# A two-layer graph network kernel: Wf's loads and W's rows in another order, and background work that passes a transposition waiting for banks

## The chip, the cores and the metric

The kernel runs on one core of one Trainium2 chip. The metric is the device time of one execution in microseconds; a kernel's time is the median of several runs.

## The reference

x has 2708 rows of 1024 float32 values, adj is a 2708 x 2708 matrix of int32. All weights are 1024 x 1024, and all arithmetic is float32.

```python
# layer 0
h = jnp.maximum(_layernorm(x, axis=-1), 0.0)
f = h @ Wf + bf
g = h @ Wg + bg
e = jax.nn.relu(f @ g.T)
scores = jnp.where(adj > 0, e, NEG)
attention = jax.nn.softmax(scores, axis=1)
x = x + attention @ (h @ W + bW)
# layer 1
h = jnp.maximum(_layernorm(x, axis=-1), 0.0)
hW = h @ W1
e = leaky_relu(hW @ a1 + (hW @ a2).T, 0.2)
scores = jnp.where(adj > 0, e, neg)
x = x + relu(jax.nn.softmax(scores, axis=1) @ hW)
```

## The kernel before

**Tiles and stages.** The rows are cut into tiles of 128, two tiles make a pair; there are ten pairs (0 to 9) and a unit of leftover rows (LEFT). The columns of the score matrix are cut into five panels of four tiles and some leftover columns. Every large product is made with seven products of half-sized blocks in place of eight, named M1 to M7; sums and differences of the operands are made on VectorE, and a product's result is read out of PSUM by one engine and combined.

Layer 0 doesn't make f and g apart: M = Wf Wg^T is made once, and the scores are h M h^T plus vectors. For the first panel the stages are, with the lines where their matmuls stand: transposes of Wg (L555) and Wf (L579) and M's rows (L591), 0 to 150 us; q = M times the panel's h (`project_q`, matmul at L679, results in the banks qx, qy, qz), 150 to 208 us; scores of all pairs against the panel (L1425, banks sx, sy, sz, the pair's h read back from DRAM as As), 208 to 374 us; then the next panel's q, 374 to 430 us; the softmax; the aggregate (L679 again, banks gx, gy, gz, gv, h read back as hc), 430 to 586 us; the projection with W (L1314), 588 to 636 us. The next panels and layer 1 follow.

**Background work.** While PE makes M and the first q, the other engines prepare h pair by pair. `make_pairs` puts these items for each pair into a list `later`: two normalizations (their fetch loads 16 pieces of x), one that stores the rows to hg_d (L143), the transposition (16 transposes on PE at L457 into four banks h_ps, copied by ACT to four tiles hsT), two dot products with the vector vb, and sums of hsT which are stored to hs_d. An item has a cost, a fetch, what it does, whether it takes PSUM banks, and a condition. `behind(us, psum_free)` is called in between the matmuls: it adds `us` to a credit and runs items from the head of the list while there is credit. An item that takes banks isn't run where `psum_free` is false, and then nothing behind it is either. `one` runs the head and starts the fetches of the next items. In the first q, the banks are free behind M1, M2, M7 and M4 only. `prepare_W` (L1352) puts eight items into the same list: W's rows (w_rows, loaded on ACT's queue) are summed on DVE into the operands wt_d of the projection; the layer-1 items also make dot products with a1 and a2 (the tiles wab).

**Queues.** `load` (L139) issues on SP, `store` (L143) on POOL's queue, w_rows on ACT's; each queue issues in program order and waits in that order. L45 is a helper through which all DVE and ACT work goes in a set order. r is the vector of the dot products; when a panel's four tiles are done, `columns_to_row` (L275) writes their column of r to DRAM as r_d, one float of 4 bytes at a time, on POOL's queue; the scores read it as a row. For the loads there is one pool of twelve buffers, shared by wg, wf, hsT, the mask tiles adj_i, As, hc and w_rows, taken in turn: a load waits until the last user of its buffer is done.

**Wf.** Four of Wf's eight row blocks are loaded at the start. In the loop over rows of M (L622), row i + 4 is loaded when row i is transposed, two per turn, and the pair loads of x come between on SP.

Of the kernel before, what the change touches and what calls it, by code (L numbers as in the profile page):

```python
# [57 lines left out]
def kernel(  # L58
# [21 lines left out]
    NC = D // P  # L80
# [117 lines left out]
    ahead = [5]  # L198
    spare, from_slots = [False], [False]

    def put(us, go, fetch=None, takes_psum=False, ready=None, to=later):
        to.append([us, fetch, go, takes_psum, ready])

    def one(of=None):
        of = later if of is None else of
        for it in of[:4 if of is lazy and from_slots[0] else ahead[0]]:
            if it[1]:
                it[1]()
                it[1] = None
        us, _, go = of.pop(0)[:3]  # L210
        go()
        return us

    def behind(us, psum_free=False):
        credit[0] = min(credit[0] + us, 2 * us)
        while later and credit[0] > 0 and (psum_free or not later[0][3]) and (not later[0][4] or later[0][4]()):
            credit[0] -= one()
        while spare[0] and not later and lazy and credit[0] > 0:
            credit[0] -= one(lazy)

# [220 lines left out]
    def make_pairs():  # L441
        xs, hT = {}, {}

        def fetch(q):
            xs[q] = []
            for t in units[q]:
                xs[q].append(row_halves("x"))
                load_rows_of(t, xs[q][-1], x)
# [58 lines left out]
        def bias(q, k):  # L507
            dots(q, k)
            drop(q, f"dots{k}")

        seen = {}
        def put_norms(q):
            put(2.1, lambda: normalize(xs[q][0]), lambda: fetch(q))
            put(2.1, lambda: normalize(xs[q][1]))

        put_rows = lambda q: put(0.5, lambda: rows(q))
        def put_dots(q):
            for k in range(2):
                put(1.6, lambda k=k: bias(q, k), ready=lambda: vb[0] is not None)

        todo = [0, 1, LEFT] + list(range(2, NQ))
        put_norms(todo[0])
# [97 lines left out]
    nc.hold = ("vector", "scalar")  # L620
    transposed_wg(0, ws)
    for a in range(NC):  # L622
        for i in range(2 * a, min(2 * a + 2, NC)):
            if i + 4 < NC:
                rows_of_wf[i + 4] = load_rows(wf, i + 4, "wf")
            transposed_wf(i)
        half_row_of_M(a, 0)
        if a == NH:
            dot(c0, halves(bfb), halves(bgb))
            vb = [slot(f"vb{g}") for g in range(2)]  # L630
            for g in range(2):
                spread(vb[g][:, :W], [v[:, 4 * g + j:4 * g + j + 1] for j in range(4)])
            ws = fetch_wg(1)
        bias_of_g(a, ws)
        if a == NH + 2:
            transposed_wg(1, ws)
        behind(2.0 if a < NH else 5.0, True)
        if a == 1:
            nc.hold = ()
# [610 lines left out]
    def project(l, p, G, finish, then={}, by_pair=False, rate=2.0):  # L1250
# [10 lines left out]
        start_of, join, finish = finish  # L1261

        order = (M1, M5, M2, M6, M7, M3, M4) if by_pair else (M1, M2, M5, M6, M3, M7, M4)
        ws = {m: load_W(l, m) for m in order[:2]}
        start_of([t for g in todo for t in g[:2]] + ([other] if other else []))
        def left_of(ta, tb, one, two):
            (a11, a12), (a21, a22) = one, two
# [84 lines left out]
    def prepare_W():  # L1352
        ab, rows = [], {}

        def fetch(l, k):
            if l == 1 and not ab:
                for k2, a in enumerate((a1, a2)):
                    row_to_all(a, wab[k2])
                ab.extend(halves(t) for t in wab)
            rows[l, k] = [load_rows(w_in[l], c, "w_rows", by_scalar) for c in (k, k + NH)]  # L1360

        def go(l, k):
            two = rows.pop((l, k))
            if l == 1:
                for i, c in enumerate((k, k + NH)):
                    for j in range(2):
                        dot(wa[:, j, c:c + 1], halves(two[i]), ab[j])
            right_of_W(l, k, *two)

        for l in range(2):  # L1370
            for k in range(NH):
                put(2.7 if l == 0 else 8.0, lambda l=l, k=k: go(l, k), lambda l=l, k=k: fetch(l, k))

    def spread_wa():
        for k in range(2):
# [156 lines left out]
    def softmax(p, S, m):  # L1532

        w = width[p]
        mb, sm = slot("mb"), slot("sm")
        spread(mb, columns_of(p, m))

        def step(q, k):
            s = S[units[q][k]]
            sub(s[:, :w], s[:, :w], mb[:, :w])  # L1540
            nc.scalar.activation(s[:, :w], s[:, :w], AF.Exp)

        order = order_of_units
        exps[0] = 0

        def go(i):
            if i < len(order):
                step(*order[i])
            if i >= LAG:
                q, k = order[i - LAG]  # L1550
                total(p, sm, S[units[q][k]], once(q, k), i == LAG)
            exps[0] += 1
        later[:0] = [[1.4, None, (lambda i=i: go(i)), False, None] for i in range(len(order) + LAG)]
        return sm

    def shifts1(p, between=None):
# [211 lines left out]
    for p in range(NP):  # L1768
        got["S"], got["acc"] = scores(p, B)
        generated[p] = NQ + 1  # L1770
        ahead[0] = 2
        S = got["S"]
        hooks = {M1: lambda p=p: take_max(p), M2: lambda p=p: take_softmax(p)}
        if p == 0:
            hooks[M1] = lambda: (held(take_max, 0), sums_may.__setitem__(0, True), sums_until(3))
        if p + 1 < NP:
            B = project_q(p + 1, hooks)
        else:
            nc.hold = ("vector",)
            project(0, p - 1, G.pop(p - 1), finish0(p - 1), hooks)  # L1780
            nc.hold = ()
            scores_before()
        then = {M4: lambda: (sums_until(NQ), prepare_W())} if p == 0 else {}
        ahead[0] = 1 if p == 0 else 2
        if p == NP - 2:
            then[M2] = lambda: first_masks(NP - 1, 0)
            then[M6] = lambda: first_masks(NP - 1, 1)
            then[M7] = lambda: first_masks(NP - 1, 2)
        spare[0], from_slots[0] = p > 0, p == NP - 1
        G[p] = aggregate(0, p, S, got["sm"], then)  # L1790
        spare[0] = False
        if p == 0:
            flush()
            ahead[0] = 2
            for s in range(1, NP):
                columns_to_row(r_d[s], s, r_[:, first_col[s]:])
            spread_wa()
        if p < NP - 2:
            project(0, p, G.pop(p), finish0(p), {M1: lambda p=p: first_masks(p + 1, 0),
                                                 M5: lambda p=p: first_masks(p + 1, 1),  # L1800
                                                 M7: lambda p=p: first_masks(p + 1, 2)})
# [4 lines left out]
    def weights1(p, z, m, shift):  # L1806
# [46 lines left out]
        for i in range(len(order) + LAG):  # L1853
            mk = []
            front.append([2.1, (lambda i=i, mk=mk: mk.append(load_mask(p, *order[i])))
                          if i < len(order) and not (p == 0 and units[order[i][0]][order[i][1]] in before) else None,
                          (lambda i=i, mk=mk: go(i, mk)), False, None])
        later[:0] = front
        return S, sm

# [89 lines left out]
```

## Time and profile before

| what | us |
|---|---|
| time, median of 3 runs | 3054.39 (3045.55 to 3057.21) |
| the profiled execution | 3049.19 |
| its span | 3047.3 |
| PE busy in the span | 2993.9 |
| DVE busy | 2047.6 |
| ACT busy | 536.8 |
| POOL busy | 496.9 |

The profile is of one execution, with a time of its own between the runs above. PE is TensorE's matmuls, DVE VectorE, ACT ScalarE, POOL GpSimd and SP the engine that only issues loads. A timeline line has a start and a duration in us, the engine, the line of the code, the operation with the tile written and the tiles read, and in brackets how long the engine had been idle and what ended that. A windows line has, for a stretch of time, the sum and the busy time of PE, its weight loads, DVE, ACT and POOL (with the number of instructions), the granted clock, the share of time in which the DMA engines were busy, and GB/s. A chain of waits is followed back from an instruction to what released it.

### The profile page before, as it was taken

How to read it: one execution, taken by the hardware profiler on the slowest of the kernel's cores; microseconds unless marked ns; L12 is line 12 of the kernel's file. 1: busy time of each engine (PE TensorE's matmuls, PEld its weight loads, DVE VectorE, ACT ScalarE, POOL GpSimd, SP SyncE). 2: the span in 40 equal slices, each digit the busy share in tenths (PEclk: the TensorE clock that was granted, in tenths of full speed). 3: DMA queues.
4: the chain of work that ended last, by engine and by line, in shares of the span. 5: the costliest groups of instructions: out<-in, count | busy, mean ns of one | idle time of the engine just before them, and what ended most of it. 6: DMA issues, size and time to landing. Idle time of an engine off the chain costs nothing.

```text
span 3047.3 us, 41722 instructions
## 1 busy us (share of the span) xinstructions
PE 2993.9 (98%) x14642; PEld 2294.2 (75%) x14642; DVE 2047.6 (67%) x4667; ACT 536.8 (18%) x880; POOL 496.9 (16%) x770
## 2 busy tenths in 40 slices
PE   8998999999999999999999999999999999999999
PEld 4576777667877588885888886784767959879695
DVE  5776794585742686616965276867878768887863
ACT  4420020020200121101210111302232121212200
POOL 1421111210112110223111111131212010020201
PEclk9999999999999999999999999999999999999999
DMA  6989878887466786768957588679768768878887
GB/s 232 302 271 272 311 276 308 264 286 235 133 236 165 228 273 195 247 156 251 292 188 251 179 241 258 223 292 335 245 212 264 263 202 299 294 265 297 264 294 268
DMA packets 392704, 766.78 MB, mean 252 GB/s; under 512 B 65728, under 2 KB 206944, under 8 KB 392464
## 3 DMA queue, kind: packets, MB, share of 16 engines
q1 hardware_dynamic: 332336, 584.80, 59.6%
q0 software_dynamic: 54464, 164.78, 16.1%
q10 hardware_dynamic: 5696, 14.55, 1.4%
q8 instruction: 116, 1.90, 0.2%
q14 instruction: 92, 0.75, 0.1%
HBM read 630.04 MB, written 138.11 MB: 252 GB/s over the span
## 4 chain that ended last, share of the span: by engine, by line
PE 73%; DVE 11%; issue 8%; DMA 5%; POOL 1%; ACT 1%; SPq 1%; POOLq 0%; DVEq 0%; ACTq 0%
PE sz L1425 6%; PE gy L679 6%; PE gz L679 6%; PE gz L1114 5%; PE gx L679 5%; PE sx L1425 4%; PE pz L1314 4%; PE sy L1425 4%; PE px L1314 4%; PE py L1314 3%; PE gy L1114 3%; PE gx L1114 3%; PE gv L679 3%; PE M_ps L591 3%; PE qz L679 2%
## 5 line engine op out<-in xcount | busy, mean ns | idle before, releaser
L1425 PE MATMUL sz<-B,As 128*128 128x288 f32 (+2 forms) x1200 | 292.0, 392 | 6.0 <-DVE st L45 5.1
L1425 PEld LDWEIGHTS sz<-B,As 128*128 128x128 f32 x1200 | 227.2, 190 | 55.2 <-DVE st L45 8.4
L1425 PE MATMUL sx<-B,As 128*128 128x288 f32 (+2 forms) x800 | 200.8, 394 | 12.4 <-DMA As<-hs_d 10.4
L1425 PE MATMUL sy<-B,As 128*128 128x288 f32 (+2 forms) x800 | 199.0, 392 | 0.0
L1425 PEld LDWEIGHTS sx<-B,As 128*128 128x128 f32 x800 | 152.5, 191 | 45.8 <-DMA As<-hs_d 9.5
L679 PE MATMUL gz<-Sa,hc 128*128 128x288 f32 (+2 forms) x800 | 185.8, 392 | 0.0
L679 PEld LDWEIGHTS gz<-Sa,hc 128*128 128x128 f32 x800 | 151.5, 190 | 32.2 <-issue 2.2
L1425 PEld LDWEIGHTS sy<-B,As 128*128 128x128 f32 x800 | 151.7, 190 | 30.6 <-DVE st L45 0.3
L1114 PE MATMUL gz<-quarter,hc 128*128 128x128 f32 (+2 forms) x1344 | 168.8, 279 | 3.8 <-DVE gT L45 3.7
L1114 PEld LDWEIGHTS gz<-quarter,hc 128*128 128x128 f32 x1344 | 160.6, 191 | 5.1 <-DVE gT L45 4.6
L143 POOL DMA_DIRECT2D out_dram<-x_res x164 | 81.2, 502 | 469.1 <-DVE x_res L45 461.9
L1314 PE MATMUL py<-w,ps 128*128 128x512 f32 x320 | 142.0, 593 | 0.0
L1314 PE MATMUL pz<-w,ps 128*128 128x512 f32 x320 | 142.0, 594 | 0.0
L1314 PE MATMUL px<-w,gT 128*128 128x512 f32 x320 | 141.1, 593 | 0.0
L679 PE MATMUL gy<-T,hc 128*128 128x288 f32 (+2 forms) x480 | 114.9, 402 | 3.8 <-DMA hc<-hg_d 3.8
L1314 PEld LDWEIGHTS pz<-w,ps 128*128 128x128 f32 x320 | 60.2, 190 | 76.2 <-issue 72.2
L1314 PEld LDWEIGHTS py<-w,ps 128*128 128x128 f32 x320 | 60.5, 190 | 75.1 <-issue 72.7
L591 PE MATMUL M_ps<-wgT,wfT 128*128 128x512 f32 x256 | 112.7, 596 | 1.6 <-ACT hsT L45 1.6
L1314 PEld LDWEIGHTS px<-w,gT 128*128 128x128 f32 x320 | 60.1, 190 | 71.3 <-issue 67.8
L679 PEld LDWEIGHTS gy<-T,hc 128*128 128x128 f32 x480 | 93.1, 194 | 24.7 <-DMA hc<-hg_d 4.3
L143 POOL DMA_DIRECT2D mk_d<-mask x55 | 35.9, 654 | 456.4 <-DVE mask L45 439.4
L45 ACT ACTIVATE P<-P 128x576 f32<-128x576 f32 (+3 forms) x111 | 72.1, 650 | 207.3 <-DVE P L45 207.2
(391 smaller groups left out, 5819.6 us busy)
## 6 DMA issues: line engine op xcount, KB each, us to landing
hc<-hg_d SPq DMA_DIRECT2D x175, 512.0 KB
As<-hs_d SPq DMA_DIRECT2D x150, 512.0 KB
hc<-hr_d SPq DMA_DIRECT2D x119, 512.0 KB
hc<-hs_d SPq DMA_DIRECT2D x112, 512.0 KB
w<-wt_d SPq DMA_DIRECT2D x96, 512.0 KB
w<-in_L_gnn_W_dram SPq DMA_DIRECT2D x72, 512.0 KB
md<-md_d SPq DMA_DIRECT2D x56, 512.0 KB
adj_i<-in_adj_dram SPq DMA_DIRECT2D x200, 128.0 KB
```

What stands on the lines that cost most here:

```text
L45: i = f(*a, **k)
L143: nc.gpsimd.dma_start(a, b)
L591: nc.tensor.matmul(ps, wfT[a][c // NH][:, c % NH, :], wgT[b][c], start=(c == 0), stop=(c == NC - 1))
L679: nc.tensor.matmul(ps[d], left(m, k, d), right(m, k), start=(start and k == 0), stop=(k == K - 1), skip_group_check=True)
L1114: nc.tensor.matmul(ps[:, d], lhs[:, d * P:(d + 1) * P], inner_right(m, n, k), start=(start and k == 0 and d == 0), stop=(k == NK - 1), ski ...
L1314: nc.tensor.matmul(ps, left[i][m][:, k, :], w_[k], start=(start and k == 0), stop=(k == NH - 1), skip_group_check=True)
L1425: nc.tensor.matmul(ps[:n, :h], lefts[q][:, i % 2, c, :n], B[m][c // 2][:, c % 2, :h], start=(start and c == 0), stop=(c == NH - 1), skip_g ...
```

## The change

It has four parts. Rows 4 to 7 of Wf are loaded together in the first turn of the loop, and row 0 of M is made as soon as row block 0 is transposed, before row block 1. Normalizations and dot products are marked `apart`; when the head of the list takes banks and none are free, `behind` runs the first of the next seven items that is marked and has been fetched. `prepare_W` is put behind M2 of the first panel's aggregate, not M4, and its layer-0 items cost 5.4, not 2.7. The first projection loads three of its weights ahead of the x_res tiles, not two. The other lines of the diff give the items that are put in by hand the new field.

```diff
-    def put(us, go, fetch=None, takes_psum=False, ready=None, to=later):
-        to.append([us, fetch, go, takes_psum, ready])
+    def put(us, go, fetch=None, takes_psum=False, ready=None, to=later, apart=False):
+        to.append([us, fetch, go, takes_psum, ready, apart])
 
-    def one(of=None):
+    def one(of=None, n=0):
         of = later if of is None else of
         for it in of[:4 if of is lazy and from_slots[0] else ahead[0]]:
             if it[1]:
                 it[1]()
                 it[1] = None
-        us, _, go = of.pop(0)[:3]
+        us, _, go = of.pop(n)[:3]
         go()
         return us
 
     def behind(us, psum_free=False):
         credit[0] = min(credit[0] + us, 2 * us)
-        while later and credit[0] > 0 and (psum_free or not later[0][3]) and (not later[0][4] or later[0][4]()):
-            credit[0] -= one()
+        while later and credit[0] > 0:
+            may = lambda it: (psum_free or not it[3]) and (not it[4] or it[4]())
+            n = 0
+            if later[0][3] and not may(later[0]):
+                n = next((i for i, it in enumerate(later[:7]) if it[5]), 0)
+                if n == 0 or later[n][1]:
+                    break
+            if not may(later[n]):
+                break
+            credit[0] -= one(n=n)
...
         def put_norms(q):
-            put(2.1, lambda: normalize(xs[q][0]), lambda: fetch(q))
-            put(2.1, lambda: normalize(xs[q][1]))
+            put(2.1, lambda: normalize(xs[q][0]), lambda: fetch(q), apart=True)
+            put(2.1, lambda: normalize(xs[q][1]), apart=True)
...
-                put(1.6, lambda k=k: bias(q, k), ready=lambda: vb[0] is not None)
+                put(1.6, lambda k=k: bias(q, k), ready=lambda: vb[0] is not None, apart=True)
...
     for a in range(NC):
+        if a == 0:
+            for i in range(4, NC):
+                rows_of_wf[i] = load_rows(wf, i, "wf")
         for i in range(2 * a, min(2 * a + 2, NC)):
-            if i + 4 < NC:
-                rows_of_wf[i + 4] = load_rows(wf, i + 4, "wf")
             transposed_wf(i)
-        half_row_of_M(a, 0)
+            if a == i:
+                half_row_of_M(a, 0)
+        if a:
+            half_row_of_M(a, 0)
...
-        ws = {m: load_W(l, m) for m in order[:2]}
+        ws = {m: load_W(l, m) for m in order[:3 if l == 0 and p == 0 else 2]}
...
-                put(2.7 if l == 0 else 8.0, lambda l=l, k=k: go(l, k), lambda l=l, k=k: fetch(l, k))
+                put(5.4 if l == 0 else 8.0, lambda l=l, k=k: go(l, k), lambda l=l, k=k: fetch(l, k))
...
-        then = {M4: lambda: (sums_until(NQ), prepare_W())} if p == 0 else {}
+        then = {M2: lambda: (sums_until(NQ), prepare_W())} if p == 0 else {}
```

More of the change, by code (lines that the diff above doesn't have):

```diff
@@ L1552, in go @@
             exps[0] += 1
-        later[:0] = [[1.4, None, (lambda i=i: go(i)), False, None] for i in range(len(order) + LAG)]
+        later[:0] = [[1.4, None, (lambda i=i: go(i)), False, None, False] for i in range(len(order) + LAG)]
         return sm
@@ L1856, in weights1 @@
                           if i < len(order) and not (p == 0 and units[order[i][0]][order[i][1]] in before) else None,
-                          (lambda i=i, mk=mk: go(i, mk)), False, None])
+                          (lambda i=i, mk=mk: go(i, mk)), False, None, False])
         later[:0] = front
```

## The prediction, made before the changed kernel had run

> **What bounds the kernel now.** I read the page first, then the waits of PE, then the places of the longest waits in the timeline, then DVE and SP around them.
>
> ```profile
> PE 2993.9 (98%) x14642; PEld 2294.2 (75%) x14642; DVE 2047.6 (67%) x4667; ACT 536.8 (18%) x880; POOL 496.9 (16%) x770
> PE 73%; DVE 11%; issue 8%; DMA 5%; POOL 1%; ACT 1%; SPq 1%; POOLq 0%; DVEq 0%; ACTq 0%
> PE sx L1425 <- DMA As<-hs_d: 10.4, 2, 9.0
> PE gy L679 <- DMA hc<-hg_d: 3.8, 1, 3.8
> PE wT_ps L579 <- DMA wf<-in_L_gnn_Wf_dram: 3.0, 2, 1.8
> PE wT_ps L579 <- ACT x L45: 1.1, 1, 1.1
> ```
>
> PE is busy in 2993.9 of 3047.3 us, so all its idle time is 53.4 us, and the change takes no matmul away. Whatever it gains is one of these waits and the slow clock after it. The last four lines (reason, total, times, longest) are the ones that the change can touch.
>
> ```profile
> 39.33 1.06 PE L579 MATMUL wT_ps<-ident,wf 128*128 128x128 f32 x8 [1.22 <-DMA wf<-in_L_gnn_Wf_dram]
> 41.45 1.94 PE L579 MATMUL wT_ps<-ident,wf 128*128 128x128 f32 x8 [1.05 <-ACT x L45]
> 43.18 14.69 PE L591 MATMUL M_ps<-wgT,wfT 128*128 128x512 f32 x32
> 182.87 7.92 PE L679 MATMUL qy<-hT,ms 128*128 128x288 f32 x32
> 235.51 2.10 PE L1425 MATMUL sy<-B,As 128*128 128x288 f32 x8
> 246.61 3.65 PE L1425 MATMUL sx<-B,As 128*128 128x288 f32 x8 [9.00 <-DMA As<-hs_d]
> 489.58 4.15 PE L679 MATMUL gv<-Sb,hc 128*128 128x288 f32 x16
> 513.06 7.18 PE L679 MATMUL gy<-T,hc 128*128 128x288 f32 x16 [3.81 <-DMA hc<-hg_d]
> ```
>
> Start, duration, what, and in brackets the idle time. Three places wait: Wf's last rows at 39 and 41, the third pair of the scores at 246, the last group of M5 in the aggregate at 513. After each the same matmuls run slower (3.65 against 2.10, 7.18 against 4.15). The line at 182.87 doesn't wait in this kernel; it is where I expect the change to make a new wait.
>
> ```profile
> 176.11 1.51 DVE L45 TENSOR_TENSOR m<-qy,m 128x288 f32<-128x288 f32 x4
> 197.76 1.28 DVE L45 BATCH_NORM_STATS2 bn<-x 128x6 f32<-128x512 f32 x2
> 181.92 7.40 SPq L139 DMA_DIRECT2D x<-in_x_dram  x16
> 140.00:150.00 10.00, 10.00 (x36) 5.31 (x35) 7.24 (x21) 4.53 (x9) 5.08 (x9) 1.00 1.05 407
> 150.00:160.00 10.00, 10.00 (x51) 8.16 (x50) 9.07 (x17) 6.25 (x12) 2.71 (x5) 1.00 1.03 187
> ```
>
> The first reads M5 out of the four qy banks; the second normalizes pair 8's first tile; the third loads pair 8. The windows end in GB/s: 407, and 187 after r_d's 4-byte column was issued at 146.72. In the chain of waits before 246.61:
>
> ```profile
> 219.45 0.76 POOL r_d L275
> 220.20 4.72 issue
> 224.95 0.50 POOL hs_d L143
> 225.48 9.64 DMA hs_d<-hsT
> 240.20 6.37 DMA As<-hs_d
> ```
>
> r_d lies between pair 7's stores, the last of them takes 9.64 us, SP then loads masks into the buffer it frees, and only then As.
>
> **What the Trainium skill says.** "TensorE: Matmul & The Clock Gate", section "What's actually happening": after an idle window of about 3.4 us the array runs at half clock until about 3.4 us of work. The trace agrees: the 9.00 us wait costs 1.55 more, the 3.81 us one 3.03 more. "DMA: Bandwidth & Descriptors", section "Specifications": below 512 B a DMA does a read-modify-write. The two r_d writes that I looked at alone landed 10.4 and 11.7 us after their issue, and in the windows 221 to 224 us, just after another, nothing moves at all (0 GB/s).
>
> **The change part by part**, against the profiled execution (3049.19 us; the median shown, 3054.39, is 5.2 above it).
>
> *Wf and M's first row.* Rows 4 to 7 are asked for 16 x loads earlier, so the waits 1.22 and 1.05 go, and with them the slow clock: 1.94 - 1.06 = 0.88 for eight transposes, 14.69 - 13.90 = 0.79 for 32 matmuls (13.90 is the same group later). Sum -3.9 at 58 us. Row 0 starts some 2 us sooner, which is lost at row 2: its copy on ACT still waits for the normalization. The 1.64 us wait for hsT near 70 stays.
>
> *Background work in the first q.* The instruction orders of both programs, side by side, show what passes. Pair 8's two normalizations and the dots of 6 and 7 run while pair 6's transposition waits for banks; pair 7's transposition moves from the scores into q's M4, pair 8 takes pair 7's place, pair 9 comes two slots earlier. On DVE, which runs in order, pair 8's first BATCH_NORM now stands between the second and third of the four reads of qy (176.11). But pair 8's loads keep their place on SP, behind two mask sets: 181.92 to 189.3. Eight loads fill its first tile, the last issued at 185.1. SP rotates through eight semaphores and the ninth load goes 3.7 us after the first, so a load needs at most 3.7 us: the tile is there by 188. From its second BATCH_NORM to rs takes 1.8 us (198.36 to 200.12 in the trace), the third read 0.46: 190.3. PE wants that bank for M3's third part at 182.87 + 2 x 1.94 = 186.75, with the 3.9 gained at 182.8. It idles 7.5 us: the 3.9 are gone, the q is 3.55 later than before, and the slow clock adds 1.55 as at 246.61. Three unknowns. r_d3 moves from 219.45 to some 175 (it needs the dots of 7, and these ACT's normalization, which ends at 173.60), just before these loads: 0 to 8 us (the dip after 146.72 lasts from 150 to 158); I take 2, as its elements may pass before 182. SP may run ahead with M: 0 to -3.9; DMA is full from 160 to 176 (over 400 GB/s), so I take -1.5. Pair 7's four hsT sums enter DVE's crowded end of q (6.00 of 6 us busy at 200 to 206): 0 to 3, taken 1. Sum for the q: 3.55 + 1.55 + 2 - 1.5 + 1 = +6.6 (bounds 0 and +16). The 16 transposes themselves only move.
>
> The 16 x loads of pair 9 and eight mask loads now stand ahead of the first As load on SP (193.33): at 0.46 us each it goes out near 205 and lands near 211, before a start of scores that is itself 6.6 later than 208.6. No cost.
>
> *The wait at 246.61.* As of the third pair now waits for pair 8's stores and masks. These stand where pair 7's stood, without r_d between them: the 4.72 us gap and part of the 9.64 go, As lands some 4 us nearer to its need. Gain 4.1; the 1.39 us wait at 278.62 goes too (its mask buffer was loaded long before). But r_d4 moves from 260.8 to between pair 9's stores, close to this As load: 0 to 8 back, I take 1.5. Sum -4.0 (bounds -11.9, all of 9.00 + 1.55 + 1.39, and 0).
>
> *W's rows.* Three items of layer 0 now run in 477 to 486, where DVE is idle (18.93 us before 490.93) and DMA moves 213 GB/s in 475 to 494. M5's third hc group takes a buffer whose wt_d store is then done; the last group reuses an hc buffer of M4, free at 487. The SP wait of 10.0 us on wt_d goes, and so 3.81 + 3.03 = -6.8. Cover needed: hc at the third group by 501; I expect its issue near 491. The new order puts layer 1's first products, which wait for wab (SP, now near 491), ahead of the four reads of gv; gz needs their banks at 513, they should end near 503. If wab came 10 us late, 2 or 3 us would be lost.
>
> *Third weight of the first project ahead of x_res; one more field per item.* PE has no wait there (588 to 636): 0.
>
> Sum: 6.6 - 4.0 - 6.8 = -4.2, so 3045.0 for an execution like the profiled one and, 5.2 higher like the median, **3050**. Everything after 640 us has the same instruction order in both programs.
>
> **The rivals.**
> 1. *No new wait in q.* Pair 8 lands early because SP moves up with M and r_d3 has passed. For it: SP is held there only by landings. Against: DMA is full until 176. Then the q keeps 3.9 - 1.5, the score waits go whole, and W's rows bring 6.8: -21, 3033.
> 2. *W's rows don't do what they should.* Stores of 6 to 10 us still hold M5's hc, or DVE waits for wab. For it: 8 waits on wt_d make 42.7 us on SP. Then +6.6 - 4.0 = +2.6, 3057.
> 3. *Slower: r_d3 stands in front of pair 8's loads.* Its write-out slows all queues, the tile lands at 196, DVE stands with two qy banks unread and PE with it: q +16 (3.55 + 1.55 + 8 + 3), and r_d4 does to the third pair what r_d3 did: 0. With W's rows +9.3, 3064; with r_d's full landing time (12.4 us is the longest shown) 3068, and over 3070 if W's rows bring less. It decides from a landing of the tile near 193, where the q's loss passes 10.8. For it: 187 GB/s after 146.72. Against: r_d2 delayed x loads, but no PE wait shows there.
>
> **How the numbers follow.** Chances: forecast 0.51 (its own range 3043 to 3058), rival 1 0.17, rival 2 0.10, rival 3 0.22. The range 3035 to 3067 leaves out most of rival 1 and the upper half of rival 3, two in ten. A measurement can tell about 0.5%, 15.3 us, from no change: below 3039.1 is faster, above 3069.7 slower. Faster is rival 1, 0.17; slower is the upper part of rival 3 and a little of 2 with it, 0.12; the rest, 0.71, is within.
>
> **What would show it.** A PE wait of 5 to 9 us at qy of L679 near 183 to 190, put down to DVE, whose own wait before a BATCH_NORM names x's load: if it is missing, rival 1. The waits at 39, 41, 278 and 513 gone; 3 to 6 us left at the third pair's sx. If gy at M5's end still waits for hc, W's rows failed. If the tile's BATCH_NORM starts after 193, rival 3. I am wrong altogether if the spans differ after 640 us.

## The result, and the profile after

The changed kernel takes 3060.49 us (median of 18 runs, 3057.09 to 3068.68), the kernel before 3052.35 us, timed beside it (18 runs, 3043.4 to 3058.41). The ratio is 1.0035, 95% interval 1.0027 to 1.0044: slower by 0.3 to 0.4%, under the 0.5% that the prediction called a difference, and against the sign of its forecast. The profiled executions show it larger: their spans are 3059.4 and 3047.3 us, 12.1 apart, because before's profiled execution (3049.19 us) lies 3.2 us below its median and the changed kernel's (3061.47 us) 1.0 us above. What follows accounts for the 12.1 us.

The page of the changed kernel, its busy times, and then its waits of PE (reason, total, times, longest):

```profile
PE 2999.2 (98%) x14642; PEld 2297.0 (75%) x14642; DVE 2048.2 (67%) x4667; ACT 536.4 (18%) x880; POOL 495.4 (16%) x770
```

```profile
PE qy L691 <- DVE m L45: 9.2, 1, 9.2
PE sx L1437 <- DMA As<-hs_d: 7.6, 1, 7.6
PE pz L1326 <- DMA w<-wt_d: 5.2, 1, 5.2
```

The same 14642 matmuls are 5.3 us longer busy, most of it because PE works 24.2 us at half its clock instead of 15.1, and PE is idle 60.2 us instead of 53.4: 5.3 + 6.8 = 12.1. Wf's and hc's waits have left the list, As's stays nearly as it was, and two are new: qy on DVE in the first q, and pz on a weight in the first project. PE's timeline of the changed kernel at these places (line numbers are 8 to 12 higher than before):

```profile
178.76 4.04 PE L691 MATMUL qy<-hT,ms 128*128 128x288 f32 x16
192.00 7.09 PE L691 MATMUL qy<-hT,ms 128*128 128x288 f32 x16 [9.19 <-DVE m L45]
...
245.27 2.18 PE L1437 MATMUL sz<-B,As 128*128 128x288 f32 x8 [1.50 <-DMA As<-hs_d]
...
256.97 4.18 PE L1437 MATMUL sx<-B,As 128*128 128x288 f32 x8 [7.58 <-DMA As<-hs_d]
260.94 4.98 PE L1437 MATMUL sz<-B,As 128*128 128x288 f32 x16
...
502.65 19.56 PE L691 MATMUL gy<-T,hc 128*128 128x288 f32 x80
...
617.72 8.80 PE L1326 MATMUL pz<-w,ps 128*128 128x512 f32 x16 [5.21 <-DMA w<-wt_d]
```

The two qy lines hold the same 16 matmuls: 4.04 us, and 7.09 after 9.19 us of idling. At 502.65 the 80 matmuls of M5 run in one piece, where before stopped for 3.81 us. Each matmul set against the same one of before gives the ledger. The offset is how many us later than in before a matmul ends; the step is what the stage added to it:

| stage | offset at its end | step | predicted step |
|---|---|---|---|
| Wf and M's first row, 58 us | -4.1 | -4.1 | -3.9 |
| first q (its end; the score part of the moved transposes taken out) | +8.3 | +12.4 | +10.5 (3.9 + 6.6) |
| scores, to the place of the old wait at 278 | +8.5 | +0.2 | -4.0 |
| to 471 us | +9.1 | +0.6 | 0 |
| W's rows, M5 in the aggregate | +2.0 | -7.1 | -6.8 |
| rest of the aggregate | +3.3 | +1.4 | 0 |
| first project, 588 to 640 us | +10.7 | +7.3 | 0 |
| everything later | +12.1 | +1.4 | 0 |

A step of one or two us is within what two traces of the same code differ by: at 58 us, the seven kernels below that leave Wf's part as it was lie -1.8 to +1.0 us from before.

What DVE, SP and POOL do around the first wait in the changed kernel:

```profile
173.91 0.79 DVE L45 TENSOR_TENSOR m<-qy,m 128x288 f32<-128x288 f32 x2
188.92 0.69 DVE L45 BATCH_NORM_STATS2 bn<-x 128x6 f32<-128x512 f32 x1 [14.23 <-DMA x<-in_x_dram]
...
191.49 0.81 DVE L45 TENSOR_TENSOR m<-qy,m 128x288 f32<-128x288 f32 x2
```

```profile
174.60 9.84 SPq L139 DMA_DIRECT2D adj_i<-in_adj_dram  x4
184.54 14.95 SPq L139 DMA_DIRECT2D x<-in_x_dram  x32
```

```profile
174.32 0.76 POOL L283 DMA_DIRECT2D r_d<-r  x1 [0.97 <-DVE mask L45]
...
243.89 0.97 POOL L283 DMA_DIRECT2D r_d<-r  x1 [7.15 <-DVE r L45]
```

DVE reads two of the four qy banks, then stands 14.23 us at pair 8's BATCH_NORM for x, and only then reads the other two; PE has no bank meanwhile. SP asks for these x (x(8) from here on) at 184.54, behind a set of four mask loads that took it 9.84 us (5.14 in before). The set follows r_d3's store, the first r_d line, by 0.3 us; r_d3 and r_d4 are the columns of r for the fourth and fifth panel. The second r_d line is r_d4's store, 1.8 us ahead of the third pair's As loads at 245.65. The stretches in the changed kernel (length, busy times with counts, PE clock, DMA share, and GB/s last):

```profile
180.00:190.00 10.00, 2.80 (x12) 1.87 (x10) 0.89 (x2) 0.00 (x0) 0.00 (x0) 0.89 0.56 108
245.00:250.00 5.00, 4.12 (x16) 2.96 (x16) 4.97 (x15) 0.00 (x0) 2.14 (x4) 1.00 0.85 81
250.00:255.00 5.00, 0.00 (x0) 0.00 (x0) 1.91 (x4) 0.00 (x0) 0.55 (x1) 0.76 0.89 87
```

After r_d4 the queues are busy (0.85 and 0.89) and yet move only 81 and 87 GB/s; the ten us ahead of them had 384 and 251. And SP's timeline of the changed kernel between the aggregate and the project, then two lines of before:

```profile
540.57 24.61 SPq L139 DMA_DIRECT2D hc<-hg_d  x4
...
575.72 23.81 SPq L139 DMA_DIRECT2D x_res<-in_x_dram  x32
...
612.35 1.00 SPq L139 DMA_DIRECT2D w<-wt_d  x2
```

```profile
558.83 20.88 SPq L139 DMA_DIRECT2D x_res<-in_x_dram  x32
...
590.60 3.12 SPq L139 DMA_DIRECT2D w<-wt_d  x2
```

The four hc loads take 24.61 us, 22.8 of it a wait for the store of W's rows; in before x_res starts at 558.83 and the second pair of wt_d weights is asked for at 590.60, not at 612.35. Everything behind that wait is 17 us late or more, and pz's weights with it.

### The profile page after: what moved, and what is told of

It is laid out like the page before. It is cut to its first block, busy times and chain, and to the rows that moved or that the text cites. A ratio compares the mean times of both kernels' runs of the same rounds, so it can differ in the third digit from the quotient of the medians.

```text
span 3059.4 us, 41725 instructions
## 1 busy us (share of the span) xinstructions
PE 2999.2 (98%) x14642; PEld 2297.0 (75%) x14642; DVE 2048.2 (67%) x4667; ACT 536.4 (18%) x880; POOL 495.4 (16%) x770
## 4 chain that ended last, share of the span: by engine, by line
PE 64%; issue 14%; DVE 12%; DMA 6%; POOL 2%; ACT 1%; SPq 1%; POOLq 0%; DVEq 0%; ACTq 0%
PE gy L691 6%; PE gz L691 5%; PE sz L1437 5%; PE gz L1126 5%; PE gx L691 5%; PE px L1326 4%; PE pz L1326 4%; PE sy L1437 3%; PE sx L1437 3%; PE py L1326 3%; PE gx L1126 3%; PE gy L1126 3%; PE gv L691 3%; DVE P L45 2%; DMA x<-in_x_dram 2%
```

## Experiments

All runs are timed beside the kernel before, and each ratio is to it. "Before" and "after" name the kernel that an experiment starts from; lines left out of an edit are marked with three dots.

**The change in four parts.** Each part alone, on before. First Wf's loads and M's first row:

```
+        if a == 0:
+            for i in range(4, NC):
+                rows_of_wf[i] = load_rows(wf, i, "wf")
...
-            if i + 4 < NC:
-                rows_of_wf[i + 4] = load_rows(wf, i + 4, "wf")
             transposed_wf(i)
+            if a == i:
+                half_row_of_M(a, 0)
-        half_row_of_M(a, 0)
+        if a:
+            half_row_of_M(a, 0)
```

> The kernel before with Wf's loads and M's first row alone. Theory 1 (DMA sets the pace from 140 to 180 us and the first As load stays put): PE is 4.1 us earlier from 58 to about 206 us, then waits at the start of the scores or longer at the third pair (about 12 us instead of 9.00); 0 to -1.5 us in all. Theory 2 (DMA follows PE): the 4.1 us last to the end, ratio 0.9987, and the wait at the third pair stays near 9.

3047.17 us, ratio 0.9995 (0.9986 to 1.0003). The offset is -3.4 at 58 us and -4.1 at 2199 us, with As's 9.0 us at sx become 3.6 at sz and 2.9 at sy. In layer 1 this execution loses the gain again: PE waits 2.7 us at gy for hc at 2197.60, which before doesn't show, half clock follows there and once more at 2433 us, and the end is at +1.8. This execution (3050.99 us) is 3.8 us above the median of its kernel, and why hc is late there stays open.

The passing alone:

```
+                n = next((i for i, it in enumerate(later[:7]) if it[5]), 0)
+                if n == 0 or later[n][1]:
+                    break
...
+            put(2.1, lambda: normalize(xs[q][0]), lambda: fetch(q), apart=True)
+            put(2.1, lambda: normalize(xs[q][1]), apart=True)
...
+                put(1.6, lambda k=k: bias(q, k), ready=lambda: vb[0] is not None, apart=True)
```

> The kernel before with the passing of background work alone. Theory 1 (DVE stands at pair 8's normalization until its x has landed, with two of the four qy banks unread): PE waits 4 to 6 us at qy near 187, the scores start some 7 us later (moved transposes apart), the third pair still waits 7 to 9: +5 to +9 us, ratio 1.002 to 1.003. Theory 2 (the wait of the changed kernel comes from the earlier Wf loads, which make PE arrive early): no wait at qy, the third pair's wait shrinks by 4: -4 us.

3062.4 us, ratio 1.0047 (1.0032 to 1.0061). PE's timeline of this kernel:

```profile
195.18 6.41 PE L687 MATMUL qy<-hT,ms 128*128 128x288 f32 x16 [9.15 <-DVE m L45]
...
259.90 0.82 PE L1433 MATMUL sx<-B,As 128*128 128x288 f32 x1 [8.22 <-DMA As<-hs_d]
```

The new wait is there with nothing else changed, and As's wait, which should have shrunk, is 8.22 us: the passing makes the whole loss of the q and gets nothing back.

W's rows alone, at M2 and at the higher cost:

```
-                put(2.7 if l == 0 else 8.0, lambda l=l, k=k: go(l, k), lambda l=l, k=k: fetch(l, k))
+                put(5.4 if l == 0 else 8.0, lambda l=l, k=k: go(l, k), lambda l=l, k=k: fetch(l, k))
...
-        then = {M4: lambda: (sums_until(NQ), prepare_W())} if p == 0 else {}
+        then = {M2: lambda: (sums_until(NQ), prepare_W())} if p == 0 else {}
```

> The kernel before with prepare_W behind M2 and cost 5.4 alone, weights in their old order. Theory 1 (DVE stands 16 us for wab, the last wt_d stores come 13 us late, SP stands behind an hc load for them, the project's loads are late): the 7 us at 513 are gained, a new PE wait of 4 to 6 us for w<-wt_d stands near 607 although the third weight is not moved: -2 to +2 us. Theory 2 (the third weight's place makes the project's wait): no wait in the project, -6 us, ratio 0.998.

3055.98 us, ratio 1.0016 (1.0009 to 1.0023). The wait at 513 us is gone, the offset is -7.9 at 518 us, and PE's timeline has the project's wait, here one product sooner:

```profile
604.04 9.24 PE L1314 MATMUL py<-w,ps 128*128 128x512 f32 x16 [7.10 <-DMA w<-wt_d]
```

The offset is +4.1 at the project's end: W's rows alone bring the project's wait.

The third weight alone:

```
-        ws = {m: load_W(l, m) for m in order[:2]}
+        ws = {m: load_W(l, m) for m in order[:3 if l == 0 and p == 0 else 2]}
```

> The kernel before with three weights ahead of x_res in the first project alone. Theory 1: the stores of wt_d are done by 552, SP loses nothing: 0 +- 1 us. Theory 2 (the load of the third weight holds SP, x_res and the fourth weight come late): a PE wait of about 5 us for w<-wt_d near 609 and +5 to +7 us.

3048.84 us, ratio 0.9993 (0.9985 to 1.0002), no wait in the project. The weight is not what makes pz wait.

**Which of the passing items does it.** After with the dots not marked. Nothing passes any more: in DVE's timeline pair 8's normalization stands behind the reads of qy again, at 193.37 us, and r_d3 between pair 7's stores, as in before:

```
-                put(1.6, lambda k=k: bias(q, k), ready=lambda: vb[0] is not None, apart=True)
+                put(1.6, lambda k=k: bias(q, k), ready=lambda: vb[0] is not None)
```

> The changed kernel with the dot products not marked, so that in effect nothing passes the transposition in the first q: r_d3 stays between pair 7's stores and pair 8's normalization behind the reads of qy. Theory 1: the 9.2 us wait at qy is gone, the third pair waits about 9 to 13 us again, the project's wait for wt_d stays; 6 to 9 us faster than the changed kernel, and pair 8's x loads leave SP some 4 us earlier than 184.5. Theory 2 (r_d3 has nothing to do with the loads): they leave at the same time as in the changed kernel.

3049.83 us, ratio 1.0004 (0.9994 to 1.0014). No wait at qy; SP's mask set takes 4.02 us and x(8) is asked for at 180.89, 3.7 us sooner than in after and 1.0 sooner than in before: there the queue does run ahead with M. The third pair waits 9.48 us and pz 3.3.

After with pair 8's and 9's normalizations held in program order on DVE (`call` runs its function as it is):

```
-            put(2.1, lambda: normalize(xs[q][0]), lambda: fetch(q), apart=True)
-            put(2.1, lambda: normalize(xs[q][1]), apart=True)
+            put(2.1, lambda: (held if q >= 8 else call)(normalize, xs[q][0]), lambda: fetch(q), apart=True)
+            put(2.1, lambda: (held if q >= 8 else call)(normalize, xs[q][1]), apart=True)
```

> The changed kernel with pair 8's and 9's normalizations held in the program's order on DVE: they come after the four reads of qy, all loads and stores keep their order, r_d3 stays early. Theory 1 (head of DVE's queue): no PE wait at qy, scores start 12 us earlier than in the changed kernel, the third pair then waits longer, since pair 8's stores and masks are tied to DMA; 5 to 12 us faster than the changed kernel. Theory 2 (r_d3 slows everything, PE waits for something else just after): another PE wait of 5 us or more appears in q, less than 4 us gained.

3059.14 us, ratio 1.0031 (1.002 to 1.0043). The wait at qy goes and another takes its place, by PE's timeline:

```profile
193.45 4.04 PE L465 MATMUL h_ps<-ident,x 128*128 128x128 f32 x16 [5.89 <-DVE u L45]
```

The normalization now stands behind qy's reads and ahead of later ones, whose banks pair 6's transposition waits for. The scores start 6.4 us late instead of 10.05. Theory 2 was right: moving the place where DVE stands isn't enough; x is not there yet.

**Is x late by the queue's order or by r_d3?** After with pair 8's loads ahead of the second mask set:

```
+    def masks_and_fetch():
+        first_masks(0, 0)
+        it = next(it for it in later if it[1])
+        it[1]()
+        it[1] = None
+
-    B = project_q(0, {M1: lambda: first_masks(0, 0), M2: lambda: first_masks(0, 1), M7: lambda: first_masks(0, 2)})
+    B = project_q(0, {M1: masks_and_fetch, M2: lambda: first_masks(0, 1), M7: lambda: first_masks(0, 2)})
```

> After with pair 8's loads moved on SP in front of the second mask set (they were behind it), nothing else moved. Theory 1, PE's wait at qy is DVE's wait for x(8): x(8) is issued near 174 to 176 us, its BATCH_NORM comes before or near 181 instead of 188.9, the 9.2 us wait at qy falls under 3 us, the scores start 6 to 9 us earlier than in after and the kernel gains about 5 us on it, or less where the masks that are now late hold DVE. Theory 2, whatever is behind r_d3 on SP comes late (10 us instead of 5) and DVE stands at the masks' use instead: a wait of 4 us or more remains in the q, named adj_i or adj_t at DVE, and the gain is under 2 us.

3068.65 us, ratio 1.0057 (1.0045 to 1.0069): worse than after. SP's and DVE's timelines of this kernel:

```profile
175.52 13.93 SPq L139 DMA_DIRECT2D x<-in_x_dram  x16
189.55 1.98 SPq L139 DMA_DIRECT2D adj_i<-in_adj_dram  x4
```

```profile
186.80 0.69 DVE L45 BATCH_NORM_STATS2 bn<-x 128x6 f32<-128x512 f32 x1 [15.79 <-DMA x<-in_x_dram]
```

Asked for 9 us sooner, the 16 loads take 13.93 us instead of 7.4 and the tile is there only 2.1 us sooner. The masks follow, DVE reads qy behind both, and PE stands 17.8 us. The edit moved more than SP's order: x(8) being fetched sooner, pair 8's normalization passes sooner too and stands ahead of all four reads of qy, so the longer time is not a price of the loads' place alone. What the run does show is theory 2's first half: what SP issues just behind r_d3 is late, masks or x. That r_d3 makes it late is not shown by it.

After with r_d3's store in another shape (order and number of instructions unchanged):

```
-        nc.gpsimd.dma_start(row[0:1, :W].rearrange("o (i p) -> p (o i)", p=P), col[:, :F])
+        nc.gpsimd.dma_start(row[0:1, :W].rearrange("o (p i) -> p (o i)" if p == 3 else "o (i p) -> p (o i)", p=P), col[:, :F])
```

> After with one store written in another shape: r_d3 goes out as 128 pieces of 4 neighbouring floats instead of 512 single floats (the row's columns are then permuted, so the third row block's bias is not the reference's); order and number of instructions are unchanged. Theory 1, the small pieces of r_d3 (issued at 174.3 us in after) hold up SP's mask set behind it (9.84 us in after, 4.0 us where no r_d was near it) and with it pair 8's loads: the mask set takes 4 to 7 us, x(8) is issued near 179 to 181, PE's wait at qy falls from 9.2 to between 2 and 5 us, and the kernel gains 4 to 7 us on after. Theory 2, the wait comes from the queue order alone (x(8) stands behind the masks, DVE behind x(8)): mask set and wait stay within 1.5 us of after's, and so does the time.

3059.04 us, ratio 1.0028 (1.0018 to 1.0037). SP's timeline of this kernel:

```profile
176.60 4.93 SPq L139 DMA_DIRECT2D adj_i<-in_adj_dram  x4
181.62 14.86 SPq L139 DMA_DIRECT2D x<-in_x_dram  x32
```

The mask set takes 4.93 us instead of 9.84 and the wait at qy is 6.5 instead of 9.2 us. If that is r_d3's shape, it accounts for 2.7 us of that wait, and the order (DVE stands at x before it reads qy) for the rest. In the time no difference from after is shown: the intervals overlap.

**The third pair: r_d4.** After with r_d3 and r_d4 in pieces of four floats, read back in that order:

```
-        nc.gpsimd.dma_start(row[0:1, :W].rearrange("o (i p) -> p (o i)", p=P), col[:, :F])
+        nc.gpsimd.dma_start(row[0:1, :W].rearrange("o (p i) -> p (o i)" if p > 2 else "o (i p) -> p (o i)", p=P), col[:, :F])
...
+        def add_rb(o, x, n, s):
+            if p > 2:
+                three = lambda v: v.rearrange("a (i j) -> a i j", j=P)
+                add(three(o), three(x), rb[:n, :W].rearrange("a (j i) -> a i j", j=P)[:, s.start // P:s.stop // P])
+            else:
+                add(o, x, rb[:n, s])
```

> After with r_d3 and r_d4 stored as 128 pieces of 4 neighbouring floats, and the row blocks' bias read back in that order (five additions read rb with a stride; the output is unchanged). Theory 1, r_d4's small pieces just before As are what kept the third pair's wait: in the windows of 5 us after r_d4's issue the DMA moves over 200 GB/s instead of 81 and 87, the third pair's waits (7.58 and 1.50 us) fall under 4 us in sum, and with r_d3's 2 us in the q (measured) the kernel gains 7 to 11 us on after. Theory 2, the wait is set by pair 9's stores and masks ahead of As on SP: the third pair still waits 7 us or more in sum, and the gain is about the 2 us of the q.

3051.72 us, ratio 1.0005 (0.9994 to 1.0016). PE's timeline of this kernel, and its stretch after r_d4's issue:

```profile
191.78 6.63 PE L691 MATMUL qy<-hT,ms 128*128 128x288 f32 x16 [8.47 <-DVE m L45]
...
250.00 2.18 PE L1444 MATMUL sx<-B,As 128*128 128x288 f32 x8 [1.66 <-DMA As<-hs_d]
```

```profile
245.00:250.00 5.00, 3.34 (x15) 2.31 (x13) 4.97 (x15) 0.00 (x0) 2.65 (x5) 1.00 0.88 170
250.00:255.00 5.00, 5.00 (x21) 3.95 (x22) 2.71 (x6) 0.00 (x0) 0.03 (x1) 1.00 1.03 421
```

170 and 421 GB/s where 81 and 87 were, and the third pair's waits for As are 1.66 instead of 7.58 + 1.50. From the start of the scores to the place of the old wait at 278 this kernel goes from +9.36 to -1.39, after from +10.05 to +8.5: 10.75 - 1.55 = 9.2 us are r_d4's. The wait at qy is 8.47 here and was 6.5 in the run before with the same r_d3, and SP's mask set takes 8.06 us here and took 4.93 there. So r_d3's share in the q is only known as 0.7 to 2.7 us of that wait, and why the mask set is slow stays open.

The same edit on before:

> Before with the same edit alone (r_d3 and r_d4 in pieces of 4 floats). Theory 1, r_d3 between pair 7's stores at 219.4 us makes the last of them slow (9.64 us to land) and so the third pair's As late: the 9.00 us wait falls under 5 us and the kernel gains 4 to 8 us on before. Theory 2, the 4.7 us that POOL stands still behind r_d, and the masks, remain: the wait stays over 7 us and the gain is under 2 us.

3047.3 us, ratio 0.9987 (0.9979 to 0.9995). PE's timeline of this kernel:

```profile
241.04 3.76 PE L1432 MATMUL sx<-B,As 128*128 128x288 f32 x8 [2.78 <-DMA As<-hs_d]
```

9.00 us have become 2.78; five other kernels that leave this stage as it was wait 5.8 to 9.6 us there. r_d3 between pair 7's stores made most of that wait in before; the change took r_d3 away from there and put r_d4 in the same position. The strided reads have a price: the 256-wide additions of rb take 600 ns instead of 412, and of the 9.3 us that this kernel is ahead at 1432 us it has 6.1 left at 1510, lost in the scores of the fourth panel, the first that r_d3's edit makes strided. By the medians it gains 2.4 us and by the ratio 4 (1.5 to 6), where 4 to 8 were expected.

**The project.** In after, DVE stood 16.45 us, until 513.63, for wab. After with a1 and a2 loaded at the start of the first aggregate:

```
-            if l == 1 and not ab:
-                for k2, a in enumerate((a1, a2)):
-                    row_to_all(a, wab[k2])
-                ab.extend(halves(t) for t in wab)
...
+        if p == 0:
+            for k2, a in enumerate((a1, a2)):
+                row_to_all(a, wab[k2])
```

> The changed kernel with a1 and a2 loaded into wab at the start of the first aggregate, not behind hc on SP. Theory 1: DVE's 16.45 us wait for wab goes, the last wt_d stores come some 10 us earlier, SP's 22.8 us wait behind hc falls below 13, the project's 5.2 us wait goes; the 7 us at 513 stay gained: 6 to 8 us faster than the changed kernel. Theory 2 (the w_rows loads themselves are what is late): DVE waits as long for w_rows, less than 2 us gained.

3060.1 us, ratio 1.0038 (1.0025 to 1.005). DVE's timeline of this kernel:

```profile
513.71 0.69 DVE L45 SCALAR_TENSOR_TENSOR junk<-w_rows,wab 128x512 bf16<-128x512 f32 x1 [14.01 <-DMA w_rows<-in_L_gnn_W_dram]
```

The product starts at 513.71, hardly later than in after, now waiting for layer 1's rows, and pz still waits 3.81 us. wab, named in after's trace, is not the cause.

Before with W's rows at M2 but the old cost of 2.7:

> Before with prepare_W put at M2 as in the change, but layer 0's rows at their old cost of 2.7. Theory 1, the higher cost is what delays layer 1's rows and the last stores (556 us in the run with both, 552 before): with 2.7 the last w_rows loads are issued by 535, SP's wait for the stores ends before 550, there is no wait for w<-wt_d in the project (7.1 us with both), the 6 to 7 us gained at 513 us stay, and the kernel is 4 to 7 us faster than before. Theory 2, the place M2 alone does it (the new order of hc's loads and stores on SP and POOL): a wait of 3 us or more for w<-wt_d stays in the project and the net is within 2 us of before.

3055.25 us, ratio 1.0018 (1.001 to 1.0026). PE's timeline:

```profile
487.79 4.12 PE L679 MATMUL gv<-Sb,hc 128*128 128x288 f32 x16 [2.64 <-DMA hc<-hg_d]
499.07 4.21 PE L971 MATMUL gv<-Sa,hl 128*128 128x288 f32 x8 [7.16 <-DMA hl<-hgl_d]
```

The project's wait is gone (last store at 544.4), as theory 1 said, but not its gain: the aggregate waits instead, for hc and for hl. hl's load goes out at 488.17 and takes 10.86 us to land, among the loads and stores of W's rows that now come sooner; that these make it late is not shown separately.

Before with layer 0's rows at M2, layer 1's left at M4:

```
-        then = {M4: lambda: (sums_until(NQ), prepare_W())} if p == 0 else {}
+        then = {M2: lambda: (sums_until(NQ), prepare_W(0)), M4: lambda: prepare_W(1)} if p == 0 else {}
```

> Before with only layer 0's rows of W put at M2 (cost 5.4), layer 1's rows left at M4. Theory 1, layer 1's rows are what comes late in the change, because they stand behind wab and the stores of layer 0 that SP waits for: left at M4 their last stores go out within 2 us of before's 551.6, x_res starts within 2 us of 558.8 less what the aggregate gained, the project waits under 1.5 us for weights, and the 6 to 7 us at 513 us stay: 4 to 7 us faster than before. Theory 2, layer 0's rows in M2 are enough to put hc's loads behind stores on SP: the wait at 513 us is gone but a wait of 3 us or more stands in the project, net within 2 us of before.

3055.82 us, ratio 1.0018 (1.001 to 1.0026); py waits 6.8 us for a weight, wab is asked for at 492.20 and the last store goes out at 555.61, as with all rows at M2 (491.69 and 556.43). Where layer 1's items enter the list is without effect, since layer 0's stand ahead of them. What is left is the cost.

Before with all at M2, layer 0's cost 5.4 and layer 1's lowered:

```
-                put(2.7 if l == 0 else 8.0, lambda l=l, k=k: go(l, k), lambda l=l, k=k: fetch(l, k))
+                put(5.4 if l == 0 else 5.3, lambda l=l, k=k: go(l, k), lambda l=l, k=k: fetch(l, k))
```

> Before with prepare_W at M2, layer 0's cost 5.4 as in the change, layer 1's cost 5.3 instead of 8.0 (the sum of the eight costs is then what it was in before). Theory 1, pacing: the last stores of W's rows go out by 546 instead of 556, x_res starts before 558, no wait of over 1.5 us for w<-wt_d in the project, the 6 to 7 us at 513 us stay, 4 to 7 us faster than before. Theory 2, SP's queue (hc loads behind w_rows' loads and wt_d's stores of the items before) sets it: the last stores still go out after 552 and a wait of 3 us or more stays in the project, or a new wait for hc or hl appears in the aggregate; net within 2 us of before, or slower.

3050.07 us, ratio 1.0001 (0.9991 to 1.001). By SP's timeline of this kernel x_res starts 18 us sooner than in after:

```profile
557.94 19.95 SPq L139 DMA_DIRECT2D x_res<-in_x_dram  x32
...
583.82 0.84 SPq L139 DMA_DIRECT2D w<-wt_d  x2
```

The last store goes out at 547.6 and no weight is waited for; 6.3 us are gained around 513 us and 4.1 lost at gz, which waits 2.1 us for hc. This kernel differs from the run of W's rows alone by layer 1's cost alone, so the pacing is what made the project wait, as theory 1 said; the gain in the time that it expected isn't there.

**Together.** Before with Wf's part, the third weight and the r_d edit:

> Before with three edits: Wf's loads and M's first row as in the change, the third weight ahead as in the change, and r_d3 and r_d4 in pieces of 4 floats; no passing, W's rows as before. If the parts add up: -4 at 58 us, carried through the q since no DVE wait is added, -4 to -8 at the third pair if r_d counts, 3.8 + 3.0 us at 513 us stay: 3038 to 3046 us, faster than before by 0.2 to 0.4%. If the earlier start only lengthens the third pair's wait and r_d doesn't count: 3047 to 3051.

3045.92 us, ratio 0.9982 (0.9974 to 0.999). The same with W's rows at M2 and costs 5.4 and 5.3:

> best_a with W's rows at M2, layer 0's cost 5.4 and layer 1's 5.3. If W's rows keep what they gain at 513 us (3.8 + 3.0): 3039 to 3042 us, 4 to 7 us under best_a's 3045.9. If a wait for hc, hl or a weight takes its place, as in the run without best_a's edits (2.1 us at gz): 3044 to 3048, the same as best_a.

3041.88 us, ratio 0.9973 (0.9964 to 0.9981), and little waiting is left in PE's timeline of this kernel at the places of the case:

```profile
237.22 2.21 PE L1436 MATMUL sx<-B,As 128*128 128x288 f32 x8 [2.10 <-DMA As<-hs_d]
250.32 2.18 PE L1436 MATMUL sz<-B,As 128*128 128x288 f32 x8 [1.39 <-DMA As<-hs_d]
498.49 4.15 PE L683 MATMUL gy<-T,hc 128*128 128x288 f32 x16 [0.18 <-DMA hc<-hg_d]
515.57 8.03 PE L683 MATMUL gz<-Sa,hc 128*128 128x288 f32 x32 [1.30 <-DMA hc<-hg_d]
```

It is faster than both kernels: all of the change but the passing, with layer 1's rows paced as fast as layer 0's and without the single-float stores of r_d3 and r_d4. Its offset is -10.7 at 278 us and -16 at 640, of which -8 is left at the end. The intervals of best_a and best_b overlap, so what W's rows add isn't shown by the times.

## Why the prediction was wrong

Between the forecast of -4.2 and the +12.1 of the traces lie 16.3 us: 7.3 in the first project, 4.2 at the third pair, 1.9 in the q's step, and the rest in steps that are small.

**Wf and M's first row** was right: -4.1 at 58 us for -3.9, and eaten in the q as the prediction says. As a price of the edit it is in part luck of the one trace: 1.7 of the 3.9 us were before's slow clock after these waits, and the kernel with the third weight alone, which waits 0.44 and 1.22 us there, shows none of it: its 32 matmuls take 13.90 us.

**Background work in the first q** had the mechanism right, place and all: DVE stands at pair 8's first BATCH_NORM between the second and third read of qy. The size was off by 1.7 us: +8.3 for +6.6. PE resumes 5.25 us later than before (192.00 against 186.75), where 3.55 and the net 0.5 of r_d3 and SP make 4.05; and the slow clock costs 7.09 - 4.04 = 3.05, where 1.55 was carried over from a wait of similar length. Pair 7's hsT sums, taken as 1 us, show nothing: 5.25 + 3.05 are the whole 8.3. SP did not run ahead by 1.5 us here: x(8) is asked for at 184.54, not at 180.4 (with Wf's part alone it is, at 180.36).

**The wait at 246.61** is the first step that failed: -4.0 predicted, +0.2 measured: 1.50 + 7.58 of waiting and 3.0 of slow clock are 12.1 us, before had 9.00 + 1.55 + 1.39 = 11.9. The term is the 1.5 us for r_d4. Its removal as a stream of single floats is worth 9.2 us. The prediction did see that r_d4 moves from 260.8 to just ahead of the third pair's As, gave 0 to 8 for it, and named the case in rival 3 ("r_d4 does to the third pair what r_d3 did"). It took a small value inside the bound although it counted 4.1 us for r_d3's leaving the same position. That position had a price in the kernel before too: of its 9.00 us, 2.78 were left when r_d3's shape changed.

**W's rows** was right where it looked: -7.1 for -6.8 at M5. It did not follow the items to the end. Four items at 5.4 instead of 2.7 spend 10.8 us more of the allowance ahead of layer 1's items, so the last store goes out at 565.2 instead of 551.6, SP stands 22.8 us in front of it, and x_res, masks and weights follow 17 us late. "PE has no wait there (588 to 636): 0", said of the third weight, was true of the kernel before and not of the changed one; that is the second step that failed, and the largest, 7.3 us. That the costs do this is shown by the three runs that vary them: 5.4 and 8.0 wait for a weight; 5.4 and 5.3 don't and pay at gz; 2.7 and 8.0 don't and pay at hl.

**Which case it was.** Rival 1 is out, the wait at qy is there. Rival 2 has one of its two signs, and without the loss: hc no longer waited on stores at M5, and DVE did stand 16.45 us for wab, but PE didn't wait for it at gz. Rival 3 has its mechanism for the third pair and not for the q: the BATCH_NORM starts at 188.92, before the 193 that it asks for. So the measured 3060.49 lies between the sums of rivals 2 and 3, and inside the range of 3035 to 3067, without either having happened as told: no rival had a wait in the project. "I am wrong altogether if the spans differ after 640 us": they do, by 1.4 us, and the clock makes it. At the same place in layer 1 both kernels wait 2.2 us, and behind it only the changed kernel's clock goes to one half, from 2443.94 to 2447.36. The same 16 matmuls in before and in the changed kernel:

```profile
2433.65 2.23 PE L1114 MATMUL gx<-T,hc 128*128 128x144 f32 x16
2444.17 3.77 PE L1126 MATMUL gx<-T,hc 128*128 128x144 f32 x16
```

The Trainium skill's "TensorE: Matmul & The Clock Gate", section "What's actually happening", names an idle window of about 3.4 us and as much work until full clock. After's trace agrees in kind: 9.19 us idle lost 3.05, and 7.58 us lost 2.08 at sx (4.18 against 2.10) and 0.94 at the sz behind it (4.98 against 4.04). It doesn't agree in size: the wait of 2.19 us above is shorter than the window, and PE worked 2.95 to 6.16 us at half clock after the longer ones. The 9.00 us of before lost only 1.55. The clock in stretches of before, and of the changed kernel (it is the third number from the end):

```profile
246.60:249.50 2.90, 2.89 (x6) 2.18 (x7) 0.00 (x0) 0.00 (x0) 0.00 (x0) 0.50 1.01 413
249.60:253.00 3.40, 3.40 (x15) 2.66 (x14) 1.54 (x4) 0.00 (x0) 0.00 (x0) 1.00 0.76 248
```

```profile
192.00:197.90 5.90, 5.90 (x12) 4.21 (x13) 5.29 (x12) 1.33 (x3) 1.08 (x2) 0.50 0.67 231
198.00:202.00 4.00, 4.00 (x24) 3.32 (x23) 1.95 (x5) 1.41 (x2) 0.30 (x1) 1.00 0.64 164
```

In both traces the granted clock is 1.00 or 0.50, and its changes lie whole multiples of 3.41 us apart: in before at 242.74, 249.57, 512.39 and 519.22, in the changed kernel at 187.73, 197.97, 252.59 and 262.83. PE came back at 246.61 and 513.06, and at 192.00 and 256.97, so it worked 2.95, 6.16, 5.97 and 5.86 us at half clock. Half of each is 1.5, 3.1, 3.0 and 2.9 us, and 1.55, 3.03, 3.05 and 3.0 were lost. So the loss went with the time from PE's return to the next return of the clock, not with the length of the wait. The 1.55 us that the prediction carried over was the cheapest of the four; its own other example, 3.03 us after a wait of 3.81, was twice that.

## What to carry to other kernels

Work that may pass a waiting item for want of PSUM can still stop PE: on an engine that runs in order, its own wait for a load stands ahead of the reads that free the banks, so ask of every item moved forward when its input lands. A stall that goes from a place usually had a cause that moves too: look where the removed transfer goes next and charge it the same price there. Follow a paced list to its last item, since what a higher cost at the head delays is the tail, and the next stage's loads queue behind it. Price the slow clock behind a wait as a range, here 1.5 to 3.1 us, and not by one example.

## What was not expected of the hardware

A store of 512 single floats (2 KB) held up some two megabytes: after r_d4 the DMA moved 81 and 87 GB/s for ten us at a share of 0.85 and 0.89, and with the same bytes in 128 pieces of 16 bytes 170 and 421, which is 2.96 MB in these ten us instead of 0.84. It was not so clear everywhere: in the q the same edit of r_d3 left the mask set at 4.93 us in one kernel and at 8.06 in another. The Trainium skill's "DMA: Bandwidth & Descriptors", section "Specifications", says that below 512 B a transfer becomes a read-modify-write; no run here shows that this is the cause, only that piece size counts far below that bound, 4 against 16 bytes. The reading side has a price too: an addition over 128x256 with one operand at a stride of four floats took 600 ns instead of 412.
